# Graph convolution on one core: the last two gathered blocks of layer 1 as plain 1 KB rows, split on ScalarE and VectorE

## The chip, the cores and the metric

The kernel runs on one core of a Trainium2 chip. The metric is the device time of one execution in microseconds. TensorE is PE in the profile, VectorE DVE, ScalarE ACT, GpSimd POOL and SyncE SP.

## What is computed

Three graph-convolution layers over 6250 nodes and 100,000 edges (sorted by destination), then a residual and a layer norm:

```python
src = concat(edge_src, arange(n)); dst = concat(edge_dst, arange(n))     # with self-loops
dinv = rsqrt(segment_sum(ones, dst))                                     # 1 / sqrt(degree)
h = x                                                                    # [6250, 256] float32
for W, b in ((W1, b1), (W2, b2), (W3, b3)):                              # 256 -> 512 -> 512 -> 256
    m = (h @ W)[src] * (dinv[src] * dinv[dst])[:, None]
    h = relu(segment_sum(m, dst, n) + b)
out = layernorm(x + h)
```

Everything is float32. TensorE multiplies in a fast float32 format of fewer bits (`F32R`), so a row is split into two parts, a high one (the row rounded to `F32R`) and a low one (row minus high part); both are multiplied and added up in the accumulator.

## The kernel before

The 6250 nodes are 50 blocks of 125. A layer first aggregates rows, scaled by `dinv`, and then multiplies by its weights. A block's aggregate comes in one of two ways. **Gathered:** 16 steps each fetch 128 rows of the layer's table in HBM by an indirect DMA on GpSimd (line 1186), and a product (line 1213) adds them up by a one-hot matrix of their destinations, which VectorE builds for four products at a time (`shot`, line 1136). A 17th set of rows, shared by ten blocks, takes what is left over. **Dense:** 50 products with a matrix of edge counts between two blocks (line 1273); the counts lie as bytes and ScalarE converts them in pieces of five (line 1145). Layer 1 does blocks 0 to 21 in the dense way and 22 to 49 by gathers, with both kinds interleaved.

How layer 1 gets high and low parts of its gathered rows: blocks 22 to 25 take plain 1 KB rows and multiply them as float32. From block 26 on (`BOTH_FROM`) the rows come from a second table, `both_halves`, which holds high and low part side by side, 2 KB per row, written at the beginning of the kernel. They land in a ring of 12 tiles, `halves` (two of which hold leftover rows), and go to TensorE as they are; a tile is free when its product is done. Layers 2 and 3 gather plain rows instead and split each behind its landing, with a copy on ScalarE (line 1240) and a subtraction on VectorE (line 1243).

The order on every engine is the order of the program text; nothing reorders it, and each engine takes its instructions in turn, waiting on semaphores. The loop in `layer` sets it: one pass per gather ("step"). In step c the gather of c is put on GpSimd's queue, then the splits of rows a few steps back (`SPLIT` has for each layer how many steps later the high part, the low part and the product come), then the product of row c - `lag`, then whatever generators are due (`go`, `go_fixed`), then the dense products that fall to this step. In layer 1 `lag` is 5.

Generators carry a block on after its last product. `after1` (layer 1) scales the sum (ScalarE line 1303, VectorE 1305), transposes it (PE 1294), copies the result (ScalarE 1314), multiplies by W1 (PE 1320), adds the bias (VectorE 1325), applies relu (ScalarE 1328) and stores the rows to layer 2's table, `tab1`, through SyncE (line 74). Layer 2's first gather on GpSimd waits for the whole of `tab1`.

The generator `teams` begins layer 2's dense part while layer 1 still runs: for groups of four blocks it streams `tab1` two blocks at a time through a ring of three loads, and the counts, through SyncE (line 76; `parts<-tab`, `parts<-kept`). For each of 150 units it splits the streamed block (ScalarE line 934, VectorE 936) and converts counts (ScalarE 926), and does four pairs of matmuls (PE line 979), one pair for each of four banks of PSUM. Its loads are put in the order when layer 1 has 16 dense products left; its first pair follows when all dense blocks are ended and the four banks are free. In layer 1 two of three pairs end a step, in layer 2 nearly each.

Of the kernel before, what the change touches and what calls it, by code (L numbers as in the profile page):

```python
# [27 lines left out]
KF = 16  # L28
CAP = KF * P
GRP = 10  # L30
# [13 lines left out]
SHORT = 6  # L44
# [7 lines left out]
FEW = 22  # L52
BOTH_FROM = 26
BOTH_LAG = 5
SPLIT = ((0, 0, BOTH_LAG), (1, 2, 8), (3, 4, 9))
EXTRAS_AFTER = (3, 6, 9, 11, 13, 15, 17)
TEAM = 4
TEAMS = 3
# [338 lines left out]
def sorted_path(ctx: ExitStack, tc: tile.TileContext, x, edges, starts, found, wts, biases, room, late, out):  # L397
# [19 lines left out]
    N, C = x.shape  # L417
    HID = w1_sb.shape[2]
    EC = d.shape[1]
    NB = N // Q  # L420
# [13 lines left out]
    src = const.tile([P, NB, KF], I32, name="ssrc")  # L434
# [285 lines left out]
    MW = -(-NB * Q // 4 // 8) * 8  # L720
# [10 lines left out]
    zt2, ht2 = [room[:, room.shape[1] - n * pair:][:, :pair].rearrange("p (k v) -> p k v", v=2 * Q) for n in (2, 1)]  # L731
    wide_rows = [room[:, at:at + HID] for at in range(MW, room.shape[1] - 2 * pair - HID + 1, HID)]
    scales = wide_rows.pop()[:, :TEAM * Q]
    del wide_rows[-TEAM:]
    at = MW + len(wide_rows) * HID
    team_zt = room[:, at:at + KH * TEAM * Q].rearrange("p (k v) -> p k v", v=TEAM * Q)
# [2 lines left out]
    turn = 0  # L739
# [305 lines left out]
    def fetch(b, chunk):  # L1045
        by_rows(nc.sync, used[len(there) % 2].rearrange("p k v -> p (k v)"), kept[b])
        there.append(chunk)
# [5 lines left out]
    def layer(i, width, gathered, dense, after, rows, first=0, spacing=1.0, extras=(), filler=None, carried=None):  # L1053
# [15 lines left out]
        items = []  # L1069
# [4 lines left out]
        total = len(items)  # L1074
# [8 lines left out]
        def go_fixed(chunk):  # L1083
            for item in list(fixed):
                if item[0] <= chunk:
                    wait = next(item[1], None)
                    if wait is None:
                        fixed.remove(item)
                    else:
                        item[0] = chunk + wait  # L1090

        def go(chunk):
            for item in list(going):
                if item[0] <= chunk + late:
                    wait = next(item[1], None)
                    if wait is None:
                        going.remove(item)
                    else:
                        item[0] = chunk + late + min(wait, item[2])
# [8 lines left out]
        def sum_bank(name, most):  # L1108
            nonlocal late
            if i == 0:  # L1110
                while not common:
                    if early_copy[0]():
                        break
                    late += 1
                    go(chunk)
                return common.popleft()
            need(now, name, most)
            return idle[name].pop(0)
# [11 lines left out]
        def more_hots():  # L1130
            c0 = len(hots) * HOTS
            n = min(HOTS, len(gathered) * (KF + 1) - c0)
            if n > 0:
                at = gathered[0] * (KF + 1) + c0
                hot = onehot.tile([P, HOTS, Q], F32R, name="shot")
                nc.vector.tensor_tensor(hot[:, :n], near_cols[:, :Q].unsqueeze(1).to_broadcast([P, n, Q]),  # L1136
                                        dlo.rearrange("p b j -> p (b j)")[:, at:at + n].unsqueeze(2).to_broadcast([P, n, Q]),
                                        op=ALU.is_equal)
                hots.append(hot)
# [9 lines left out]
        landed, split_rows = {}, {}  # L1149
        hi_lag, lo_lag, lag = SPLIT[i]  # L1150

        def of_both(c):

            n, b, _ = items[c]
            return i == 0 and (n * GRP if b is None else b) >= BOTH_FROM

        def halved(c):

            return 0 <= c < total and items[c][1] is not None and i > 0
        acc = None  # L1160

        of_ten = {}
        shared, rows = rows[:2 if i == 0 else 1], rows[2 if i == 0 else 1:]
# [3 lines left out]
        def gather(c):  # L1167
            nonlocal turn
            n, b, j = items[c]
            table = both_halves if of_both(c) else tables[i]  # L1170
            if (i, b, j) == (0, BOTH_FROM, BOTH_LAG + 1):
                hot_stores.appendleft(late_hot_room)
            if b is None:
                row, at = split.popleft() if of_both(c) else shared[n % len(shared)], rest[:, n, 0:1]
                of_ten[n] = row
                if i > 0:
                    of_ten[n] = shared_halves
                    raw_of_ten.append((c, row))
            elif of_both(c):
                row, at = split.popleft(), src[:, b, j:j + 1]  # L1180
                split_rows[c] = row
            else:
                row, at = rows[turn % len(rows)], src[:, b, j:j + 1]
                (landed if i > 0 else split_rows)[c] = row
                turn += 1
            nc.gpsimd.indirect_dma_start(out=row, out_offset=None, in_=table,  # L1186
                                         in_offset=bass.IndirectOffsetOnAxis(ap=at, axis=0))
# [39 lines left out]
        with tc.manual_schedule():  # L1227
            more_hots()
            to_sum = 0
            for chunk in range(total + (SHORT if i == 1 else lag)):  # L1230
                now = chunk
                if i == 1:
                    lag = SPLIT[i][2] if returning is None else max(SHORT, SPLIT[i][2] - (chunk - returning) // 2)
                if chunk < total:
                    gather(chunk)
                if halved(chunk - hi_lag):
                    halves = split_rows[chunk - hi_lag] = split.popleft()
                    if i == 1 and halves in loaned:
                        on_loan.append(halves)
                    nc.scalar.copy(halves[:, :width], landed[chunk - hi_lag])  # L1240
                if halved(chunk - lo_lag):
                    halves = split_rows[chunk - lo_lag]
                    nc.vector.tensor_sub(halves[:, width:], landed.pop(chunk - lo_lag), halves[:, :width].bitcast(F32))  # L1243
                while to_sum <= chunk - lag:
                    product(to_sum)
                    to_sum += 1
                if raw_of_ten and to_sum >= raw_of_ten[0][0] and chunk >= raw_of_ten[0][0] + LATE:
                    row = raw_of_ten.popleft()[1]
                    nc.scalar.copy(shared_halves[:, :width], row)
                    nc.vector.tensor_sub(shared_halves[:, width:], row, shared_halves[:, :width].bitcast(F32))  # L1250
                go(chunk)
                go_fixed(chunk)
                until = min(len(dense) * NB, begun + int((chunk + 1 - first) * NB / spacing))
                if i == 0:
                    until = min(until, done + 3)
                if chunk >= total - 1:
                    until = len(dense) * NB
                while done < until:
                    m, k = divmod(done, NB)
                    if k == 0:  # L1260
                        if chunk < total - 1 and (len(there) <= m or there[m] > chunk):
                            break
                        assert len(there) > m
                        acc_d = sum_bank(bank, 3)
                        if i == 2 and m + 1 < len(dense) and len(there) == m + 1:
                            fetch(dense[m + 1], chunk)
                    if k % PIECE == 0:
                        while len(got) < min(len(dense) * CUTS, done // PIECE + 1 + ahead):
                            n, c = divmod(len(got), CUTS)
                            if n > m and (len(there) <= n or there[n] > chunk):  # L1270
                                break
                            got.append(converted(n, c))
                    nc.tensor.matmul(acc_d[:Q], lhsT=got[done // PIECE][:, k % PIECE, :], rhs=parts[:, k],  # L1273
                                     start=(k == 0), stop=(k == NB - 1))
                    products = done = done + 1
                    if k == NB - 1:
                        finished += 1
                        ended(chunk, dense[m], acc_d, bank)
            assert all(steps_ is carried for _, steps_ in fixed)
            while going:  # L1280
                late += 1
                go(chunk)
                if carried is not None:
                    next(carried)
                if filler is not None:
                    next(filler, None)
            while filler is not None and begun % PIECE:
                next(filler)
# [389 lines left out]
```

## Time and profile before

| | |
|---|---|
| time, median of 3 runs | 2076.28 us (2072.91 to 2077.11) |
| the profiled execution, its span | 2076.16 us, 2074.4 us |
| PE, PEld, DVE busy | 1923.9 us (93%), 1513.7 us (73%), 1494.1 us (72%) |
| ACT, POOL busy | 1302.3 us (63%), 1418.2 us (68%) |
| layer 1's gathers on POOL | 72.95 to 685.66 us |
| layer 2's gathers on POOL | 708.98 to 1587.99 us |
| layer 3's gathers on POOL | 1620.7 to 2060.9 us |
| gathers from `both_halves` on POOL | 384, mean 939 ns |
| all bytes moved by DMA | 486.17 MB, mean 234 GB/s |

A row of the timeline has the start, the length, engine, line, operation, output and input with shapes, and in brackets the engine's idle time before it and what ended it; rows of one kind that follow each other are merged (x2). A matmul's length runs to the end of its passage, so lengths overlap; the work that one costs is the distance to the start of the next. In a row of busy windows the first number is the length of the stretch, then come the busy times of PE, PEld, DVE, ACT and POOL with the number of instructions, PE's granted clock, the DMA engines' share and GB/s. "SPq" is the time in which SyncE issues DMAs.

### The profile page before, as it was taken

The page shows a single profiled execution, that of the slowest core. Times are in us where ns is not written, and L with a number is a line of the kernel's source. Part 1 is how long each engine was busy: PE and PEld are TensorE (multiplying, and loading weights), DVE is VectorE, ACT ScalarE, POOL GpSimd, SP SyncE. Part 2 cuts the span into 40 slices and gives each one's busy share as a digit, 9 for nine tenths or more (in the row PEclk, how much of TensorE's full clock was granted, in tenths as well). Part 3 has the DMA queues.
Part 4 walks back from the last instruction along what each step waited for, and adds up shares of the span by engine and source line. Part 5 has one row for each costly group of instructions (what it writes and reads, how often), then busy time and mean ns, then how long its engine had stood idle before and what let it go on. Part 6 is the DMA issues. An engine that isn't in the chain of part 4 may idle for free. (4 is left out here: it accounts for less than half of the span.)

```text
span 2074.4 us, 30032 instructions
## 1 busy us (share of the span) xinstructions
PE 1923.9 (93%) x8642; PEld 1513.7 (73%) x8642; DVE 1494.1 (72%) x2809; ACT 1302.3 (63%) x2484; POOL 1418.2 (68%) x1442
## 2 busy tenths in 40 slices
PE   4399999999999688999999999999989899999996
PEld 3277777777776467778888878887767777777774
DVE  6877888888882376777766777677675467777776
ACT  2576777787884465766766656667565455556553
POOL 2467777766777377777776776677674577777775
PEclk6699999999999899999999999999999999999998
DMA  7898999999999999999999998978886466666674
GB/s 172 244 308 212 271 260 256 276 260 257 275 274 252 264 268 248 269 260 265 261 262 258 258 260 239 266 230 266 244 239 189 115 180 183 182 178 190 174 191 117
DMA packets 233624, 486.17 MB, mean 234 GB/s; under 512 B 44142, under 2 KB 87358, under 8 KB 233446
## 3 DMA queue, kind: packets, MB, share of 16 engines
q0 software_dynamic: 125184, 315.61, 54.6%
q1 hardware_dynamic: 94980, 159.23, 27.9%
q10 hardware_dynamic: 13282, 9.30, 1.7%
q8 instruction: 70, 1.15, 0.2%
q14 instruction: 108, 0.88, 0.1%
HBM read 416.51 MB, written 67.47 MB: 233 GB/s over the span
## 5 line engine op out<-in xcount | busy, mean ns | idle before, releaser
L1186 POOL DMA_INDIRECT room<-tab,ssrc x1008 | 1025.8, 1018 | 384.6 <-issue 162.6
L1243 DVE TENSOR_TENSOR halves<-room,halves 128x512 fp32r<-128x512 f32 (+1 forms) x806 | 453.4, 579 | 279.0 <-ACT halves L1240 273.0
L1240 ACT CAST halves<-room 128x512 fp32r<-128x512 f32 (+1 forms) x806 | 408.5, 528 | 286.0 <-DMA room<-tab,ssrc 244.7
L1213 PE MATMUL sacc<-halves,shot 128*125 128x512 f32 x1541 | 527.1, 406 | 38.8 <-DVE shot L1136 27.8
L1186 POOL DMA_INDIRECT halves<-both,ssrc x384 | 360.5, 939 | 143.3 <-issue 41.8
L1213 PEld LDWEIGHTS sacc<-halves,shot 128*125 128x125 f32 x1541 | 286.9, 188 | 120.4 <-ACT halves L1240 25.1
L785 DVE TENSOR_TENSOR room<-near_cols,slots 128x625 bf16<-128x625 f32 (+2 forms) x435 | 325.3, 804 | 30.8 <-PE sacc L852 12.7
L1145 ACT CAST piece<-room 125x625 fp32r<-125x625 uint8 x416 | 297.2, 722 | 70.4 <-PE win_ps L1273 19.2
L1136 DVE TENSOR_TENSOR shot<-near_cols,sdlo 128x500 fp32r<-128x500 f32 x371 | 248.0, 670 | 9.3 <-PE sacc L1213 4.8
L1366 PE MATMUL win_ps<-room,w_sb 128*128 128x250 f32 (+1 forms) x832 | 192.5, 375 | 1.6 <-ACT room L1372 1.6
L1273 PE MATMUL win_ps<-parts,piece 125*125 125x512 f32 x650 | 186.2, 405 | 6.2 <-ACT piece L1145 6.2
L1273 PE MATMUL smm<-parts,piece 125*125 125x512 f32 x655 | 188.9, 405 | 1.3 <-ACT piece L1145 0.7
L1366 PEld LDWEIGHTS win_ps<-room,w_sb 128*128 128x128 f32 x832 | 158.0, 195 | 25.3 <-ACT room L1372 2.0
L1273 PE MATMUL mat_ps<-parts,piece 125*125 125x512 f32 x600 | 172.4, 404 | 1.3 <-ACT piece L1145 1.3
L852 PEld LDWEIGHTS <-room 128*125 128x125 bf16 x725 | 95.8, 138 | 74.0 <-issue 23.0
L1273 PE MATMUL sacc<-parts,piece 125*125 125x512 f32 x450 | 147.6, 432 | 0.9 <-ACT piece L1145 0.9
L1273 PEld LDWEIGHTS win_ps<-parts,piece 125*125 125x125 f32 x650 | 119.3, 188 | 37.7 <-ACT piece L1145 8.0
L814 ACT CAST room<-sacc 125x500 uint8<-125x500 f32 (+1 forms) x155 | 107.6, 712 | 56.5 <-PE sacc L852 41.7
L1273 PEld LDWEIGHTS smm<-parts,piece 125*125 125x125 f32 x655 | 116.8, 187 | 29.3 <-issue 2.3
L936 DVE TENSOR_TENSOR parts<-parts 125x512 fp32r<-125x512 f32 x150 | 103.4, 689 | 41.6 <-ACT parts L934 41.6
L1273 PEld LDWEIGHTS mat_ps<-parts,piece 125*125 125x125 f32 x600 | 107.6, 186 | 29.4 <-ACT piece L1145 3.0
L1243 DVE TENSOR_TENSOR parts<-room,parts 128x512 fp32r<-128x512 f32 x138 | 93.4, 692 | 33.3 <-ACT parts L1240 32.9
(310 smaller groups left out, 2938.5 us busy)
## 6 DMA issues: line engine op xcount, KB each, us to landing
parts<-tab SPq DMA_DIRECT2D x81, 448.0 KB
kept<-room SPq DMA_DIRECT2D x29, 683.6 KB
room<-kept SPq DMA_DIRECT2D x29, 683.6 KB
tab<-st SPq DMA_DIRECT2D x74, 224.0 KB
room<-tab,ssrc POOLq DMA_INDIRECT x1008
both<-parts SPq DMA_DIRECT2D x10, 1120.0 KB
own_row<-tab SPq DMA_DIRECT2D x38, 224.0 KB
parts<-kept SPq DMA_DIRECT2D x60, 136.7 KB
```

The source lines that it names most:

```text
L785: nc.vector.tensor_tensor(out, near_cols[:, :shape[2]].unsqueeze(1).to_broadcast(shape), numbers.unsqueeze(2).to_broadcast(shape), op=ALU. ...
L814: nc.scalar.copy(place[:, :, u * G:(u + len(ms)) * G].rearrange("p k (t r) -> p t k r", r=G), counted_in[:Q, :len(ms) * 256].rearrange("p ...
L852: nc.tensor.matmul(bank[:Q, len(pair) * 256:][:, :G * NB], lhsT=hot_lo, rhs=hot_key, start=True, stop=True)
L936: nc.vector.tensor_sub(to[:, HID:], row, to[:, :HID].bitcast(F32))
L1136: nc.vector.tensor_tensor(hot[:, :n], near_cols[:, :Q].unsqueeze(1).to_broadcast([P, n, Q]), dlo.rearrange("p b j -> p (b j)")[:, at:at + ...
L1145: convert(piece, made_or_read[:, c * PIECE:(c + 1) * PIECE, :])
L1186: nc.gpsimd.indirect_dma_start(out=row, out_offset=None, in_=table, in_offset=bass.IndirectOffsetOnAxis(ap=at, axis=0))
L1213: nc.tensor.matmul(acc[:Q, :size], lhsT=hot, rhs=row[:, c0:c0 + size], start=(i == 1 and k == c0 == 0), stop=(k == KF and c0 + size == row ...
L1240: nc.scalar.copy(halves[:, :width], landed[chunk - hi_lag])
L1243: nc.vector.tensor_sub(halves[:, width:], landed.pop(chunk - lo_lag), halves[:, :width].bitcast(F32))
L1273: nc.tensor.matmul(acc_d[:Q], lhsT=got[done // PIECE][:, k % PIECE, :], rhs=parts[:, k], start=(k == 0), stop=(k == NB - 1))
L1366: nc.tensor.matmul(h_ps[:, f, :], lhsT=w2_sb[:, k, (f2 + f) * P:(f2 + f + 1) * P], rhs=zt[:, k, :], start=(k == 0), stop=(k == KH - 1))
```

## The change

Blocks 48 and 49 (`PLAIN_FROM`) no longer come from `both_halves`: their 32 gathers fetch plain 1 KB rows of layer 1's own table into a ring of eleven rows of their own (`plain_rows`, in space that held other things earlier in the layer), ScalarE copies the high part one step later and VectorE subtracts the low part two steps later, as in layer 2, into tiles of the same `halves` ring. Products fall back from five to eight steps behind their gather over the twelve steps ahead of block 48 and come up to six again at the end; the loop runs six steps past its last gather instead of five.

```diff
 BOTH_FROM = 26
 BOTH_LAG = 5
-SPLIT = ((0, 0, BOTH_LAG), (1, 2, 8), (3, 4, 9))
+PLAIN_FROM = 48
+SPLIT = ((1, 2, BOTH_LAG), (1, 2, 8), (3, 4, 9))
...
+    plain_rows = [room[:, at:at + C] for at in range(3 * MW, MW + len(wide_rows) * HID - C + 1, C)]
...
         def of_both(c):
             n, b, _ = items[c]
-            return i == 0 and (n * GRP if b is None else b) >= BOTH_FROM
+            return i == 0 and BOTH_FROM <= (n * GRP if b is None else b) < PLAIN_FROM
 
         def halved(c):
-            return 0 <= c < total and items[c][1] is not None and i > 0
+            return 0 <= c < total and items[c][1] is not None and (i > 0 or items[c][1] >= PLAIN_FROM)
...
             else:
-                row, at = rows[turn % len(rows)], src[:, b, j:j + 1]
-                (landed if i > 0 else split_rows)[c] = row
+                ring = plain_rows if i == 0 and b >= PLAIN_FROM else rows
+                row, at = ring[turn % len(ring)], src[:, b, j:j + 1]
+                (landed if halved(c) else split_rows)[c] = row
                 turn += 1
...
-            for chunk in range(total + (SHORT if i == 1 else lag)):
+            plain = total - (NB - PLAIN_FROM) * KF
+            for chunk in range(total + (SHORT if i < 2 else lag)):
                 now = chunk
+                if i == 0:
+                    lag = min(BOTH_LAG + max(0, chunk - plain + 12) // 4, SPLIT[1][2], SHORT + max(0, total + 1 - chunk) // 2)
```

How this moves instructions is seen at two places. Lines of the changed kernel are up to six higher: its 1246 and 1249 are the splits, 1309, 1320 and 1334 the transforms on ScalarE, 1216 the products, 1300 and 1326 transposes and W1 on PE, 928 and 936 the teams' conversions, 981 their matmuls.

ScalarE, from the last dense pieces of layer 1 to the teams' first conversions (`szs`, `room`, `st`: the blocks' transforms; `parts`: the teams'), before:

```order
L1145 CAST piece<-room 125x625 x3
L1328 ACTIVATE st<-st,sdinv 125x512 x2
L1303 ACTIVATE szs<-str,sdinv 125x256
L1314 COPY room<-sacc_877 128x250
L1303 ACTIVATE szs<-smm,sdinv 125x256
L934 CAST parts<-parts 125x512
L926 CAST parts<-parts 125x5x125 x4
L1328 ACTIVATE st<-st,sdinv 125x512
L1314 COPY room<-sacc_877 128x250
```

The same place now:

```order
L1334 ACTIVATE st<-st,sdinv 125x512
L1246 CAST halves_858<-room 128x256
L1246 CAST halves_860<-room 128x256
L1309 ACTIVATE szs<-str,sdinv 125x256
L1246 CAST halves_861<-room 128x256
L936 CAST parts<-parts 125x512
L928 CAST parts<-parts 125x5x125 x2
L1246 CAST halves_862<-room 128x256
L928 CAST parts<-parts 125x5x125 x2
L1246 CAST halves_863<-room 128x256
L1320 COPY room<-sacc_876 128x250
L936 CAST parts<-parts 125x512
```

Copies of gathered rows now stand between the transforms and between the teams' conversions; one relu has gone from behind the first conversions.

TensorE, where the teams' first pair stands (`win_ps` is block 49's sum before; now `sacc_877` is block 48's and `sacc_876` block 49's), before:

```order
L1294 MATMUL sacc_877<-ident_r,szs 128x125 x2
L1213 MATMUL win_ps<-halves_863,shot 125x512
L1213 MATMUL win_ps<-halves_864,shot 125x512
L1320 MATMUL sacc_876<-w_58,room 125x512
L979 MATMUL sacc_878<-parts 128x500 x2
L1213 MATMUL win_ps<-halves_865,shot 125x512
L1320 MATMUL sacc_876<-w_58,room 125x512
L979 MATMUL mat_ps<-parts 128x500 x2
```

And now:

```order
L1300 MATMUL sacc_876<-ident_r,szs 128x125 x2
L1216 MATMUL sacc_877<-halves_855,shot 125x512
L1216 MATMUL sacc_877<-halves_856,shot 125x512
L1326 MATMUL win_ps<-w_58,room 125x512
L981 MATMUL sacc_878<-parts 128x500 x2
L1216 MATMUL sacc_877<-halves_857,shot 125x512
L1326 MATMUL win_ps<-w_58,room 125x512
L981 MATMUL mat_ps<-parts 128x500 x2
L1216 MATMUL sacc_877<-halves_858,shot 125x512
L1216 MATMUL sacc_877<-halves_866,shot 125x512
L981 MATMUL smm<-parts 128x500 x2
L1201 MATMUL sacc_876<-parts,ident_r 125x512
```

The first pair has moved from among block 49's products to among block 48's: two products of block 48 and all sixteen of block 49 now stand behind it, where eleven of block 49 did.

## The prediction, made before the change was run

> **What bounds the kernel now.** I read the page first, then the busy windows around the change of layers, then each engine's timeline there. The profiled execution took 2076.16 us: its span of 2074.4 and 1.8 around it. The median of the three timed runs is 2076.28, so a sum made against the profiled time needs no correction. About 0.2% (4.15 us) is what a measurement of this kernel can tell from no change.
>
> ```profile
> span 2074.4 us, 30032 instructions
> ```
>
> Stretches of 5 us at the end of layer 1 and the start of layer 2 (columns: PE, PEld, DVE, ACT, POOL busy with counts; granted PE clock; DMA share; GB/s):
>
> ```profile
> 665.00:670.00 5.00, 4.62 (x22) 3.42 (x21) 1.35 (x3) 0.77 (x2) 3.78 (x5) 1.00 1.08 272
> 670.00:675.00 5.00, 3.43 (x12) 1.67 (x10) 1.48 (x3) 0.55 (x2) 3.78 (x5) 1.00 1.36 264
> 675.00:680.00 5.00, 0.79 (x1) 0.28 (x1) 0.69 (x1) 1.94 (x4) 3.78 (x5) 0.69 1.35 255
> 680.00:685.00 5.00, 2.94 (x5) 1.73 (x6) 1.28 (x2) 3.04 (x6) 1.28 (x2) 0.50 1.38 273
> ```
>
> TensorE is the bound up to 668 us. Then it starves, with the DMA engines over-booked (shares of 1.35 and more). The PE timeline says on what, and shows a second hole at 710:
>
> ```profile
> 652.27 0.40 PE L1213 MATMUL smm<-halves,shot 128*125 128x512 f32 x1
> ...
> 667.47 0.64 PE L1273 MATMUL str<-parts,piece 125*125 125x512 f32 x2
> ...
> 673.94 0.49 PE L1213 MATMUL win_ps<-halves,shot 128*125 128x512 f32 x1 [1.00 <-DMA halves<-both,ssrc]
> 677.01 0.79 PE L1213 MATMUL win_ps<-halves,shot 128*125 128x512 f32 x1 [2.57 <-DMA halves<-both,ssrc]
> 682.05 2.07 PE L1320 MATMUL sacc<-w,room 128*125 128x512 f32 x2 [4.26 <-ACT room L1314]
> 683.14 1.82 PE L979 MATMUL sacc<-parts 125*128 125x500 f32 x2
> ...
> 695.91 0.63 PE L1213 MATMUL win_ps<-halves,shot 128*125 128x512 f32 x2
> ...
> 708.85 0.61 PE L979 MATMUL smm<-parts 125*128 125x500 f32 x2
> 709.30 0.62 PE L979 MATMUL str<-parts 125*128 125x500 f32 x2
> 718.98 1.51 PE L979 MATMUL sacc<-parts 125*128 125x500 f32 x2 [9.05 <-ACT parts L934]
> ```
>
> 652.27 is the first product of the 32 gathers that change, 667.47 the last of layer 1's dense products, 683.14 the first matmul of the teams (they begin layer 2's dense part early), 695.91 layer 1's last product. POOL's rows give those gathers, from 641.68 to 685.66:
>
> ```profile
> 641.68 0.94 POOL L1186 DMA_INDIRECT halves<-both,ssrc  x1 [0.30 <-issue]
> 642.92 0.94 POOL L1186 DMA_INDIRECT halves<-both,ssrc  x1 [0.31 <-PE win_ps L1273]
> ...
> 666.97 0.94 POOL L1186 DMA_INDIRECT halves<-both,ssrc  x1 [0.30 <-PE smm L1213]
> 668.22 0.94 POOL L1186 DMA_INDIRECT halves<-both,ssrc  x1 [0.31 <-PE str L1273]
> ...
> 685.66 0.94 POOL L1186 DMA_INDIRECT halves<-both,ssrc  x1 [3.47 <-DMA parts<-tab]
> 708.98 0.96 POOL L1186 DMA_INDIRECT room<-tab,rest  x1 [22.39 <-DMA tab<-st]
> ```
>
> The two products that waited for DMA belong, by count, to the gathers of 666.97 and 668.22: 7.0 and 8.8 us from issue to use. Layer 2's first gather, 708.98, waits for the last store of layer 1's table. What lies between 678 and 709 is on ScalarE and SyncE:
>
> ```profile
> 678.06 0.62 ACT L934 CAST parts<-parts 125x512 fp32r<-125x512 f32 x1 [7.45 <-DMA parts<-tab]
> 678.58 2.55 ACT L926 CAST parts<-parts 125x625 fp32r<-125x625 uint8 x4
> 681.04 0.71 ACT L1328 ACTIVATE st<-st,sdinv 125x512 f32<-125x512 f32 x1
> 681.66 0.34 ACT L1314 COPY room<-sacc 128x250 f32<-128x250 f32 x1
> ```
>
> ```profile
> 664.48 4.19 SPq L76 DMA_DIRECT2D parts<-kept  x8
> 668.72 4.31 SPq L76 DMA_DIRECT2D parts<-tab  x6
> ```
>
> So the chain is: SyncE issues the teams' loads from 664.48; the first load of layer 1's table (issued 668.72) lands only at 678.06; ScalarE stands before it for 7.45 us, then converts four pieces (2.46), and only behind these comes the copy (681.66) for which TensorE waits until 682.05. From 683.14 TensorE works through to the last product at 695.91. From that product to layer 2's first gather it is 13.1 us.
>
> **The change part by part.** *Bytes.* At a gather every 1.24 us (641.68, 642.92), 128 rows of 2 KB are 211 GB/s; with 1 KB rows half of that, 4.2 MB less in all. From 664.48 to 678.06 the teams' loads (8 transfers of counts, 0.61 MB, then 0.50 MB of the table) moved 1.11 MB, 82 GB/s. With 264 GB/s in all (row of 670) and 105 for gathers, 159 are left, and the 1.11 MB take 7.0 us: landing at 671.5. That leaves out the table's own stores, which SyncE issues just ahead of the loads; two of them (0.26 MB each, 125 rows of 2 KB) make it 1.63 MB and 674. Nothing reaches much below 670.8, for the load is issued only at 668.72 (0.7 us sooner at best) and the shortest passage that I find, below, is 2.8 us. At the other end, 678.06 stays if halved rows relieve nothing. I take 672.5, between the two that come from the rows of this very stretch.
>
> Whether rows of half the length take half of the engines' time, two other layers tell (2 KB rows at 1000 us, 1 KB rows at 1700 us), and the row of 1500 is for later:
>
> ```profile
> 1000.00:1050.00 50.00, 50.00 (x229) 41.97 (x228) 37.14 (x61) 33.30 (x60) 36.77 (x36) 1.00 0.92 254
> 1500.00:1550.00 50.00, 40.48 (x164) 31.52 (x163) 38.63 (x62) 32.25 (x61) 36.80 (x36) 0.90 0.88 250
> 1700.00:1750.00 50.00, 50.00 (x217) 39.89 (x215) 36.37 (x97) 27.73 (x66) 38.42 (x39) 1.00 0.70 184
> ```
>
> A full share would be 276 GB/s in the one and 263 in the other, so nearly by the byte. The Trainium skill ("DMA: Bandwidth & Descriptors", section "Anatomy of one DMA — SWDGE (gpsimd) path") speaks against the change here: a transfer issued by GpSimd costs a fixed 2.0 us and only its bytes at 436 GB/s on top. By that rule, as an estimate, a gather of 0.26 MB goes from 2.6 to 2.3 us; if that is the engines' time, their load falls by 12% and not by half, the teams' load lands about when it did, and the time is that of the second rival (2081.9) instead of 2074.4. The two rows speak against reading the fixed part as time that the engines are taken.
>
> *Splits.* There are 32 copies on ScalarE and 32 subtractions on VectorE more. Layer 3 has the same instructions:
>
> ```profile
> L1243 DVE TENSOR_TENSOR halves<-room,halves 128x256 fp32r<-128x256 f32 x336 | 136.1, 420 | 110.2 <-ACT halves L1240 108.4 <-PE mat_ps L1273 0.7 <-PE smm L1273 0.5
> L1240 ACT CAST halves<-room 128x256 fp32r<-128x256 f32 x336 | 126.9, 401 | 100.3 <-DMA room<-tab,ssrc 89.2 <-DVE halves L1243 5.3 <-DVE szs L1412 1.7
> ```
>
> That is 12.8 us on ScalarE and 13.4 on VectorE over some 45 us in which they are idle for more than half (0.55 to 3.04 and 0.69 to 1.48 of 5 us): the busy time costs nothing. What could cost is their order. ScalarE takes row c one step behind its gather, so everything behind it on ScalarE (pieces L1145 for the dense products, the transforms L1303, L1314, L1328) and on VectorE (the one-hots L1136, L1325) now waits for that row. How late a 1 KB row can be, layer 3 shows: a gather in its middle and its last one, and the copies for which ScalarE waited for them (paired by counting):
>
> ```profile
> 1801.17 1.01 POOL L1186 DMA_INDIRECT room<-tab,ssrc  x1 [0.30 <-DVE szs L1411]
> ...
> 2060.90 0.95 POOL L1186 DMA_INDIRECT room<-tab,ssrc  x1 [0.30 <-issue]
> ```
>
> ```profile
> 1808.46 0.41 ACT L1240 CAST halves<-room 128x256 fp32r<-128x256 f32 x1 [2.79 <-DMA room<-tab,ssrc]
> ...
> 2063.72 0.41 ACT L1240 CAST halves<-room 128x256 fp32r<-128x256 f32 x1 [0.82 <-DMA room<-tab,ssrc]
> ```
>
> So 7.3 us in traffic and 2.8 at the end without. A one-hot made at step c stands behind the subtraction of row c-2, so TensorE's step c comes no sooner than issue(c) - 2.5 + 2.8 to 7.3 + 0.40 + 0.42 + 0.67, that is 1.8 to 6.3 us behind the gather. TensorE is behind it by more already: at 652.27 it is in the sixth of these steps, whose gather was issued at 641.68 + 5 x 1.24 = 647.9 (4.4 us), at 667.47 in the sixteenth, issued at 660.3 (7.2 us). Only at the beginning, and only with late rows, does 6.3 exceed 4.4: some 2 us at most, which then stay, as TensorE has no slack up to 668. Against it, products eight steps behind instead of five put three of them (0.23 each) behind the dense end, 0.7 us sooner there. I set the two against each other: 0 (bounds -0.7 and +2).
>
> *POOL.* It no longer waits for a free row of the split ring: the plain rows have a ring of eleven of their own, free once subtracted. Its last gather moves from 685.66 to about 641.68 + 31 x 1.24 = 680.2, and a landing of 7.3 still brings the row before 688. That is before TensorE gets to it, so it gains nothing.
>
> *Order.* The teams start earlier in the order, and more of their work stands ahead of the last product: counted in PE's order, 23 pairs of L979 between the first and the last product against 16, 21 products against 12, and two L1320 more. A pair is 0.45 us (708.85, 709.30), a product 0.23, an L1320 0.46: 3.2 + 2.1 + 0.9 = 6.2 us more. ScalarE's way from the landed load to the first pair was 683.14 - 678.06 = 5.1; it loses one L1328 (0.62) and gains two copies (0.80): 5.3. So the last product comes at 672.5 + 5.3 + (695.91 - 683.14) + 6.2 = 696.8, against 695.91. Layer 2 starts 0.9 us later, within -0.8 and +2.4 by the bounds of the landing (670.8 and 674).
>
> What is won is work. By PE's order 63 pairs against 54 stand ahead of layer 2's first product, and TensorE now waits for that product anyway (9.05 us at 709.30). So 9 pairs, 9 x 0.45 = 4.1 us, leave layer 2, where each step carries about one pair until the teams end. All of it counts where TensorE never idles (the row of 1000: 50.00 of 50), nothing where it idles more than that (the row of 1500, just behind the teams' end: 40.48 of 50). Between 0 and 4.1 I take 2.7, nearer to the row without idle time, since most of the teams' steps lie in such stretches.
>
> *Sum.* 2076.16 + 0.9 (start of layer 2) - 2.7 (pairs) = **2074.4**. Bounds: -0.8 - 4.1 gives 2071.3, +2.4 with nothing from the pairs 2078.6.
>
> **The rivals.** *Everything lands well (2068.9).* The first load lands at 670.8 (start of layer 2 -0.8), all nine pairs count (-4.1), and the clock stays up: 683.14 to 695.91 is 12.8 us for 10.4 us of work (16 pairs, 12 products, one L1320), so 2.4 us went to the lowered clock (0.50 in the row of 680). If the products that now come at the gathers' pace of 1.24 us keep TensorE awake, they come back. 2076.16 - 0.8 - 4.1 - 2.4 = 2068.9. For it: twenty products run unhindered where before they stood for DMA. Against it: one product of 0.23 us in 1.24 is little activity.
>
> *The load lands no sooner (2081.9, slower).* If the teams' first load still lands at 678.06, because the engines are as full as before, then the larger amount of work ahead of the last product is pure delay: 678.06 + 5.3 + 12.8 + 6.2 = 702.3 against 695.91, 6.4 us later. Engines so full mean late rows too, so the 2 us of the splits come with it; the pairs give back 2.7: 2076.16 + 6.4 + 2.0 - 2.7 = 2081.9. It decides from a landing of 674.3 on, where delay and pairs cancel. For it: shares of 1.35 to 1.38 from 670 to 685 say that far more was queued than could be served, and layer 3's landing of 7.3 us came at a mere 0.70. Against it: 105 GB/s less are asked for.
>
> **How the numbers follow.** The forecast has 0.50: by its bounds of 2071.3 to 2078.6 mostly within 0.2%, with 0.08 below 2072.0. The first rival has 0.24, all of it faster. The second has 0.26, slower (beyond 2080.3). That makes faster 0.32, same 0.42, slower 0.26. The range goes from 2067.5 (the first rival, with 1.4 for a sooner start of the loads) to 2082.0, the second rival's price; what lies beyond that price, about half of its chance, and a small part of the first are left out.
>
> **What would show it.** Right: POOL issues the 32 gathers at 1.24 to 1.31 us without a gap, the last by 682.5; ScalarE's first L936 of the teams (L934 before) starts at 671 to 674 instead of 678.06; the first pair comes near 678 and the last product near 697, with no wait for gathered rows on PE between; layer 2's first gather is within 2 us of 708.98; the teams' last pair comes some 2 to 4 us sooner than before. Wrong: a ScalarE wait for a gathered row of over 5 us ahead of a piece or a transform, dense products that end later than 669, or a first load that lands behind 674.3. I would be wrong altogether if layer 2 then took another course, since its order against the teams shifts by nine pairs.

## The result, and the profile after

The changed kernel takes 2091.22 us (median; 2088.54 to 2101.12) where the kernel before takes 2076.19 in the same measurement: a ratio of 1.0083, 95% interval 1.0067 to 1.0099. It is slower, and outside the forecast's range. The profiled execution took 2093.96 us.

```profile
span 2092.3 us, 30116 instructions
```

First the end of layer 1, at which the prediction looked. The four stretches of 5 us again, of the changed kernel:

```profile
665.00:670.00 5.00, 4.61 (x21) 3.23 (x19) 3.74 (x8) 2.46 (x6) 3.78 (x5) 1.00 0.89 244
670.00:675.00 5.00, 0.15 (x1) 0.00 (x0) 0.00 (x0) 1.80 (x4) 3.78 (x5) 0.94 1.05 254
675.00:680.00 5.00, 2.80 (x5) 1.59 (x6) 3.45 (x7) 4.29 (x12) 3.78 (x5) 0.50 1.05 253
680.00:685.00 5.00, 5.00 (x19) 3.55 (x18) 3.17 (x7) 2.68 (x7) 2.35 (x3) 0.88 1.04 289
```

The DMA share fell from 1.35 and more to 1.05. ScalarE's timeline (the teams' first conversion), TensorE's (last dense products, first pair, last product) and GpSimd's (first and last of the 32 gathers, layer 2's first):

```profile
673.20 0.62 ACT L936 CAST parts<-parts 125x512 fp32r<-125x512 f32 x1 [3.91 <-DMA parts<-tab]
```

```profile
667.53 0.64 PE L1279 MATMUL str<-parts,piece 125*125 125x512 f32 x2
...
678.28 1.82 PE L981 MATMUL sacc<-parts 125*128 125x500 f32 x2
...
697.81 0.63 PE L1216 MATMUL sacc<-halves,shot 128*125 128x512 f32 x2
```

```profile
642.73 0.95 POOL L1189 DMA_INDIRECT room<-tab,ssrc  x1 [0.31 <-issue]
...
682.01 0.94 POOL L1189 DMA_INDIRECT room<-tab,ssrc  x1 [0.30 <-issue]
709.03 1.04 POOL L1189 DMA_INDIRECT room<-tab,rest  x1 [26.07 <-DMA parts<-tab]
```

All of this is as predicted, and layer 2 starts at 709.03 instead of 708.98. The time is lost later, in code that the change does not touch. GpSimd's timeline at the end of layer 2's gathers, the start of layer 3's and their end:

```profile
1614.60 1.27 POOL L1189 DMA_INDIRECT room<-tab,ssrc  x1 [0.53 <-DVE halves L1249]
1641.51 0.94 POOL L1189 DMA_INDIRECT room<-tab,rest  x1 [25.64 <-issue]
...
2079.74 0.95 POOL L1189 DMA_INDIRECT room<-tab,ssrc  x1 [0.30 <-issue]
```

Layer 2's 612 gathers go from 709.03 to 1614.60, 905.6 us, against 879.0 before: 26.6 us more. The gap to layer 3 gives 5.8 back (26.9 against 32.7) and layer 3 itself 2.0 (438.2 against 440.2); with layer 2's start that is 18.8 at the last gather (2079.74 against 2060.90) and 17.9 of span.

### The profile page after: what moved, and what is told of

The parts are those of the page before. It is cut to its first block, busy times and chain, and to the rows that moved or that the text cites. A ratio compares the mean times of both kernels' runs of the same rounds, so it can differ in the third digit from the quotient of the medians.

```text
span 2092.3 us, 30116 instructions
## 1 busy us (share of the span) xinstructions
PE 1930.7 (92%) x8642; PEld 1517.6 (73%) x8642; DVE 1508.0 (72%) x2841; ACT 1313.7 (63%) x2516; POOL 1428.0 (68%) x1442
## 4 chain that ended last, share of the span: by engine, by line
PE 56%; DMA 17%; issue 9%; DVE 5%; POOL 5%; ACT 4%; SPq 1%; ACTq 0%; POOLq 0%; DVEq 0%
DMA room<-tab,ssrc 15%; PE sacc L1216 10%; PE win_ps L1279 6%; PE smm L1279 6%; PE mat_ps L1279 5%; POOL room L1189 5%; PE sacc L1279 5%; PE win_ps L1372 4%; PE win_ps L1385 3%; PE sacc L1326 2%; DVE halves L1249 1%; PE sacc L854 1%; PE str L1279 1%; ACT halves L1246 1%; PE str L981 1%
## 5 line engine op out<-in xcount | busy, mean ns | idle before, releaser
L1189 POOL DMA_INDIRECT room<-tab,ssrc x1040 | 1066.5, 1025 | 409.5 <-issue 168.8
L1249 DVE TENSOR_TENSOR halves<-room,halves 128x512 fp32r<-128x512 f32 (+1 forms) x841 | 467.7, 573 | 302.4 <-ACT halves L1246 296.8
L1246 ACT CAST halves<-room 128x512 fp32r<-128x512 f32 (+1 forms) x841 | 422.5, 524 | 288.3 <-DMA room<-tab,ssrc 257.6
L1216 PE MATMUL sacc<-halves,shot 128*125 128x512 f32 x1581 | 544.0, 409 | 49.5 <-DVE shot L1138 36.8
L1189 POOL DMA_INDIRECT halves<-both,ssrc x352 | 330.5, 939 | 128.1 <-issue 40.3
L1216 PEld LDWEIGHTS sacc<-halves,shot 128*125 128x125 f32 x1581 | 296.2, 190 | 133.4 <-ACT halves L1246 21.8
```

The lines of the kernel that those rows point to most:

```text
L1216: nc.tensor.matmul(acc[:Q, :size], lhsT=hot, rhs=row[:, c0:c0 + size], start=(i == 1 and k == c0 == 0), stop=(k == KF and c0 + size == row ...
```

## Experiments

Ratios are against the kernel before, each with its 95% interval. The traces come from several chips, so times are compared through the ratios. A = changed kernel, B = kernel before.

**Which part of the change does it?** Two things pass from layer 1 into layer 2: the teams stand nine pairs further on, and the ring of gathered rows begins at another row.

*hold5*: A with the teams' first pair put back.

```diff
         half(1, 1)
+        yield 5
         pairs_done = 0
```

> The changed kernel with the teams' first pair held back by five steps, so that 54 pairs stand ahead of layer 2's first product and 16 ahead of layer 1's last, as in the kernel before (the changed kernel: 63 and 23). Theory A (the loss in layer 2 comes from the teams standing nine pairs further on against layer 2's blocks): the loss goes, 2072 to 2078 us, layer 2's gathers take about 879 us from first to last. Theory B (it comes from the ring of gathered rows, which enters layer 2 at position 5 of 7 instead of 1): it stays, 2088 to 2095 us, gathers about 905 us. Theory C (contention at the end of layer 1 or of the transfers): 2088 to 2095 us too, but the next run tells it from B.

Measured: 0.9981 (0.9967 to 0.9995), 2071.87 us, a hair below theory A's range; layer 2's gathers take 875.2 us.

*a_turn* and *b_turn*: the ring's count, at the end of layer 1, put back in A and advanced in B.

```diff
 assert len(common) == 7 - TEAM
+turn -= 2 * KF      # a_turn;  in b_turn: turn += 2 * KF
```

> The changed kernel with the count of the ring of gathered rows set back by 32 before layer 2, so that layer 2 begins at the same one of its 7 rows as in the kernel before; the teams stay nine pairs ahead. Theory A (the teams' place): nothing changes, 2088 to 2095 us. Theory B (the ring's place): the loss goes, 2072 to 2080 us. Theory C: 2088 to 2095 us.

> The kernel before with the count of the ring advanced by 32 before layer 2, so that layer 2 begins at the row at which the changed kernel begins; the teams stand as before. Theory A: 2074 to 2079 us. Theory B: 2088 to 2095 us. Theory C: 2074 to 2079 us.

Measured: a_turn 1.0086 (1.0064 to 1.0108), b_turn 0.9986 (0.9969 to 1.0002). The ring has no part in it.

*b_p2*: B with the teams alone moved ahead.

```diff
-if in_layer == 0 and pairs_done % 3 or ...
+if in_layer == 0 and pairs_done % 2 or ...
```

> The kernel before with a step between the teams' pairs of layer 1 that is taken after every odd pair instead of after two of three: 66 pairs instead of 54 stand ahead of layer 2's first product and 21 instead of 16 ahead of layer 1's last. Theory A: slower, 2083 to 2095 us, with layer 2's gathers 890 us or longer. Theory B: 2072 to 2078 us, since 12 pairs leave layer 2 and 5 x 0.45 us come into layer 1's end. Theory C: 2074 to 2079 us.

Measured: 1.0103 (1.0066 to 1.0140), 2091.76 us; layer 2's gathers take 898.9 us. So a loss of this size comes without plain rows, without splits and without another lag, as soon as the teams are further on. Theory A holds, B and C fall. It does not say how.

**Is it the distance, or a phase?** Over hundreds of steps a constant distance of nine pairs should cost nothing, so I tried a phase between the teams' conversions and the blocks (theory P) against plain distance (theory M).

*a_d2* and *h5_d1*: a pause of the teams in layer 2, two steps in A, one step in hold5.

```diff
         for u, (g, k) in enumerate(units):
+            if in_layer == 1 and now >= EAGER and not paused:
+                paused = True
+                yield 2      # h5_d1: yield 1
```

> The changed kernel with the teams paused once, for two steps, at step 9 of layer 2; layer 1 stays as the change has it. The teams are then 6.6 steps ahead of where they stand in the kernel before, instead of 8.6. Theory M (the further the teams are ahead of layer 2's blocks, the more layer 2 loses): about a quarter of the loss goes, 2086 to 2090 us. Theory P (what counts is where in a block's 16 steps the teams' five-unit conversions on ScalarE fall; they come every 19.17 steps, so five of them fill six blocks at places 3.2 steps apart, and two steps bring the places back to those of before): the loss goes, 2070 to 2080 us.

> The changed kernel with the first pair held back by five steps (2071.9 us) and the teams paused once more, for one step, at step 9 of layer 2. Theory M: as fast as without the pause or faster, 2068 to 2074 us. Theory P: the conversions fall one step off, as in the changed kernel, 2084 to 2092 us.

*a_k1*: A with the conversions of counts one unit earlier. *hold9*: hold5 with nine steps.

```diff
-if k % PIECE == 2 and u + PIECE < len(units):
+if k % PIECE == 1 and u + PIECE < len(units):      # a_k1
```

> The changed kernel with the teams' five-unit conversions, and the loads of counts behind them, one unit (four pairs, 3.8 steps) earlier, and nothing else moved; the pairs stand as far ahead as the change has them. Theory M: 2088 to 2095 us. Theory P: the places in the block move by 3.8 modulo 3.2 = 0.6 step, a part of the loss goes, 2075 to 2088 us.

> The changed kernel with the first pair held back by nine steps instead of five: 48 pairs ahead of layer 2's first product. Theory M: as fast as with five or faster, 2066 to 2073 us. Theory P: the conversions fall 0.65 step off the good places, 2072 to 2085 us.

Measured: a_d2 1.0018 (1.0000 to 1.0036), h5_d1 0.9976 (0.9958 to 0.9993), a_k1 1.0102 (1.0080 to 1.0125), hold9 0.9956 (0.9940 to 0.9972; 2064.81 us). Theory P is out: only a_d2 (2078.81 us) lies in its range, while h5_d1 (2068.48) should have been slow and a_k1 (2092.53) better. Theory M does not fit either: two steps of nearly nine took away most of the loss (from 1.0083 to 1.0018). Something between them decides.

**Where the time goes.** I listed the distances between the starts of layer 2's gathers, 1.44 us in the mean before. Those over 4.5 us, by the number of the gather behind which they lie:

| kernel | ratio | distances over 4.5 us (gather: us) |
|---|---|---|
| B, hold5, h5_d1, hold9, b_turn, a_d2 | 0.9956 to 1.0018 | none |
| A | 1.0083 | 240: 6.5, 369: 7.8, 560: 5.0 |
| a_turn | 1.0086 | 240: 6.8, 369: 7.8, 560: 5.0 |
| a_k1 | 1.0102 | 17: 11.8, 240: 7.8, 369: 10.8 |
| b_p2 | 1.0103 | 21: 6.8, 182: 4.6, 439: 6.0, 560: 5.8 |

A's three places on GpSimd's timeline:

```profile
1058.46 0.94 POOL L1189 DMA_INDIRECT room<-tab,ssrc  x1 [0.94 <-DVE halves L1249]
1064.99 0.95 POOL L1189 DMA_INDIRECT room<-tab,ssrc  x1 [5.58 <-DVE halves L1249]
...
1254.28 0.94 POOL L1189 DMA_INDIRECT room<-tab,ssrc  x1 [0.87 <-DVE halves L1249]
1262.07 0.95 POOL L1189 DMA_INDIRECT room<-tab,ssrc  x1 [6.85 <-DVE parts L1249]
...
1537.74 0.95 POOL L1189 DMA_INDIRECT room<-tab,ssrc  x1 [0.30 <-issue]
1542.76 0.94 POOL L1189 DMA_INDIRECT room<-tab,ssrc  x1 [4.07 <-DVE halves L1249]
```

They exceed three ordinary distances by 15.0 us, of the 26.6 that layer 2 lost. GpSimd waits for VectorE to free a row. The timeline of all engines at the second place, in order of time, says why VectorE is late. Lines 1372 and 1378 are the products with W2 and the relu of `hidden`, the generator that carries two aggregated blocks through W2 and W3; 1352 copies a transposed block of layer 2:

```profile
1252.67 0.62 ACT L1246 CAST halves<-room 128x512 fp32r<-128x512 f32 x1 [0.82 <-DMA room<-tab,ssrc]
1253.19 0.82 ACT L1378 ACTIVATE room<-win_ps,b_sb 128x250 f32<-128x250 f32 x2
1253.32 0.69 DVE L1249 TENSOR_TENSOR halves<-room,halves 128x512 fp32r<-128x512 f32 x1 [1.29 <-ACT halves L1246]
1254.07 1.96 PE L1372 MATMUL win_ps<-room,w_sb 128*128 128x250 f32 x8 [1.62 <-ACT room L1378]
1254.28 0.94 POOL L1189 DMA_INDIRECT room<-tab,ssrc  x1 [0.87 <-DVE halves L1249]
1255.86 0.59 PE L1300 MATMUL sacc<-ident_r,szs 125*128 125x125 f32 x4
1256.29 1.86 PE L1372 MATMUL win_ps<-room,w_sb 128*128 128x250 f32 x8
1258.18 0.83 ACT L1378 ACTIVATE room<-win_ps,b_sb 128x250 f32<-128x250 f32 x2 [4.17 <-PE win_ps L1372]
1258.90 1.05 ACT L1352 COPY room<-sacc 128x500 f32<-128x500 f32 x2
1259.54 0.73 PE L1216 MATMUL sacc<-halves,shot 128*125 128x512 f32 x2 [1.39 <-ACT room L1352]
1259.83 0.64 ACT L936 CAST parts<-parts 125x512 fp32r<-125x512 f32 x1
...
1260.35 1.69 ACT L1246 CAST parts<-room 128x512 fp32r<-128x512 f32 x3
1260.51 0.69 DVE L938 TENSOR_TENSOR parts<-parts 125x512 fp32r<-125x512 f32 x1 [6.50 <-ACT parts L936]
...
1261.12 0.69 DVE L1249 TENSOR_TENSOR parts<-room,parts 128x512 fp32r<-128x512 f32 x1
...
1262.07 0.95 POOL L1189 DMA_INDIRECT room<-tab,ssrc  x1 [6.85 <-DVE parts L1249]
```

ScalarE stands for 4.17 us before a relu whose matmuls TensorE is only then doing. Behind it on ScalarE, in turn, are the copies of gathered rows (1260.35, three of them at once: they had landed). VectorE stands for 6.50 us: its next instruction needs the teams' copy (1259.83), which is in ScalarE's queue behind the relu and two copies more. Only then does it subtract a gathered row (1261.12) and so free it, and GpSimd has stood for 6.85. That ScalarE's queue is strictly first in, first out is what the Trainium skill says ("PSUM — Partial Sum Buffer", section "Engine vs sequencer instructions"), and these rows agree: nothing passed the relu in 4.17 us.

Why the relu stands so close behind its matmuls is seen in the order of the instructions. TensorE at the first of the three places, changed kernel (the timeline above, of the second, counts each W2 product twice):

```
L981 MATMUL sacc_878<-parts 128x500 x2
L1216 MATMUL sacc_877<-halves_6268,shot 125x512 x2
L1216 MATMUL sacc_877<-halves_6264,shot 125x512 x2
L1372 MATMUL win_ps<-room,w_sb 128x250 x4
L981 MATMUL mat_ps<-parts 128x500 x2
L1372 MATMUL win_ps<-room,w_sb 128x250 x4
L1300 MATMUL sacc_877<-ident_r,szs 128x125 x4
L1372 MATMUL win_ps<-room,w_sb 128x250 x8
L1216 MATMUL sacc_876<-halves_6269,shot 125x512 x2
```

An ordinary place, kernel before: between two groups of W2 products stand a gathered product and a pair.

```
L1366 MATMUL win_ps<-room,w_sb 128x250 x4
L979 MATMUL sacc_878<-parts 128x500 x2
L1213 MATMUL sacc_877<-parts,shot 125x512 x2
L1366 MATMUL win_ps<-room,w_sb 128x250 x4
L979 MATMUL mat_ps<-parts 128x500 x2
L1213 MATMUL sacc_877<-parts,shot 125x512 x2
```

In A the transforms run through several rounds with no row, product or pair between. The code does that here, when a block's first product finds no free sum bank (layer 2 has two):

```python
while held.get(name, 0) >= most:
    late += 1
    go(chunk)          # (comment added) only the transforms; no gather, no split, no pair
```

And the banks are missing because of `hidden`. The teams' results go through it, two blocks at a time, six times in all, and so do layer 2's own blocks, two every 32 steps. It has one tile for what comes out of W2, `ht2`, which a pair of blocks takes first and keeps to its end, and one window bank. Counted in the order, the teams' results come in B at steps 152, 216, 344, 408, 536 and 568, seven to nine steps behind layer 2's own (143, 208, 337, 401, 528, 560). In A they come at 143, 207, 335, 392, 527 and 554: at 207, 335 and 527 a step or two *ahead* of layer 2's own, which then wait for `ht2` (the pair of step 208 has it at 229, in B at 213) and keep `zt2`, their place ahead of it. The next block's sum waits for that place in its bank, the block after it takes the second bank, and a third finds none. The layer stands for 9, 8 and 9 steps at its steps 234, 363 and 554. GpSimd's long distances end at gathers 241, 370 and 561, seven later: there are seven rows in the ring. In hold5, h5_d1, hold9 and a_d2 the layer nowhere stands, in a_turn and a_k1 as in A, in b_p2 for 16 steps at five places (5, 1, 4, 1 and 5). I call this theory W; where the texts below speak of the one window bank, it is `ht2` and that bank together.

**Theory W tried both ways.** *a_tz11*, *a_tz17*: A, in which only the teams' six results begin later; the pairs stay nine ahead. *b_tz25*: B, in which only these come later, so that they fall just ahead of layer 2's own.

```diff
             if n == TEAM - 1:
...
-                yield SOON
+                for _ in range(11):      # a_tz17: 17;  b_tz25, in B: 25
+                    yield 1
                 team_ended[0](hidden(groups[g][:2], ...))
```

The loop takes the place of a wait of two steps, so the first result of each group comes 9, 15 and 23 steps later.

> The changed kernel with the teams' six results (hidden of two blocks at a time) begun eleven steps later, at steps 152, 216, 344, 408, 536 and 568 of layer 2 as in the kernel before, instead of 143, 207, 335, 392, 527 and 554; the pairs stay nine ahead. Theory W (at 207, 335 and 527 a team's result takes the one window bank one or two steps ahead of layer 2's own two blocks, those keep both sum banks, and the layer stands at its next block for 9, 8 and 9 steps of the order in which no row is gathered): the loss goes, 2066 to 2076 us, and the jumps at steps 240 and 370 with it. Theory M (the pairs' place itself): 2088 to 2095 us.

> The changed kernel with the teams' six results begun seventeen steps later (steps 158, 222, 350, 414, 542, 574, as they stand in the kernel held back by nine steps, 2064.8 us). Theory W: the loss goes, 2062 to 2075 us. Theory M: 2088 to 2095 us.

> The kernel before with the teams' six results begun 23 steps later and nothing else changed: they then stand at steps 175, 231, 367, 424, 559 and 587, a step or two ahead of layer 2's own pairs of blocks at 176, 369 and 560, and the layer stands for 9, 8 and 5 steps at steps 202, 395 and 586. Theory W: slower by 12 to 24 us, 2086 to 2098 us, with jumps of 4 us or more in the gathers near steps 207 and 400. Theory M: 2072 to 2079 us, since no pair moves.

Measured: a_tz11 0.9988 (0.9970 to 1.0007; 2074.06 us), a_tz17 1.0003 (0.9984 to 1.0022; 2076.73 us, a little above its range), b_tz25 1.0090 (1.0055 to 1.0124; 2093.04 us). GpSimd's waits from 709 to 1600 us (in total, number, the longest), of A:

```profile
POOL room L1189 <- DVE halves L1249: 80.8, 108, 5.6
POOL room L1189 <- DVE parts L1249: 26.7, 36, 6.9
```

and of a_tz11:

```profile
POOL room L1190 <- DVE halves L1250: 66.7, 111, 2.6
POOL room L1190 <- DVE parts L1250: 24.0, 41, 2.0
```

The long waits are gone, no distance is over 3.9 us, and layer 2's gathers take 881.2 us (GpSimd's timeline, a_tz11):

```profile
706.79 1.03 POOL L1190 DMA_INDIRECT room<-tab,rest  x1 [26.26 <-DMA parts<-tab]
...
1588.02 0.95 POOL L1190 DMA_INDIRECT room<-tab,ssrc  x1 [0.31 <-issue]
```

b_tz25 has them, at the two places that were named ahead (gathers 208 and 401) and, seven gathers behind its third stand at 586, at 592. On GpSimd's timeline:

```profile
1003.66 0.95 POOL L1187 DMA_INDIRECT room<-tab,ssrc  x1 [0.30 <-issue]
1010.35 1.15 POOL L1187 DMA_INDIRECT room<-tab,ssrc  x1 [5.75 <-DVE halves L1244]
...
1287.39 0.95 POOL L1187 DMA_INDIRECT room<-tab,ssrc  x1 [0.30 <-issue]
1294.04 1.15 POOL L1187 DMA_INDIRECT room<-tab,ssrc  x1 [5.70 <-DVE halves L1244]
...
1565.78 0.95 POOL L1187 DMA_INDIRECT room<-tab,ssrc  x1 [0.30 <-issue]
1572.22 1.15 POOL L1187 DMA_INDIRECT room<-tab,ssrc  x1 [5.49 <-DVE halves L1244]
```

A fourth, 5.8 us behind gather 463, lies at no stand; B has a lesser one there, 4.4 us.

So the kernel before can be made as slow as the changed one by the place of six results, and the changed one as fast as before. Theory M falls: no pair moved in any of the three.

*hold14*: A with the first pair fourteen steps later, to see whether more holding back gains more.

> The changed kernel with the first pair held back by fourteen steps: 42 pairs ahead of layer 2's first product and 2 ahead of layer 1's last, so that the teams' results fall clear of layer 2's own (163, 227, 355, 419, 547, 579). Theory W: no loss, and layer 1's end keeps what nine pairs fewer give it, 2060 to 2072 us. Theory M: 2060 to 2068 us, further down than with nine steps (2064.8 us).

Measured: 0.9986 (0.9965 to 1.0007), 2072.96 us, 1.0 above W's range and 5.0 above M's, and no better than hold9. By pairs ahead the kernels without a stand read 42: 0.9986, 48: 0.9956, 54: 0.9981, 63: 0.9988 (a_tz11): no trend shows. The lowest ratio of all is that of hold9, the change with the first pair nine steps later: it is faster than A and B, but its interval meets those of hold5 and hold14.

## Why the prediction was wrong, point by point

- *Bytes.* Right. The first load landed for 673.20, forecast 672.5 between 670.8 and 674. (The upper bound should have been 674.7: 1.63 MB at 159 GB/s take 10.2 us from 664.48.) Of the 4.9 us won, 1.6 come from an earlier issue, at 667.15 instead of 668.72, where the prediction saw 0.7 at best. The rest is passage: from SyncE's issue to ScalarE's first conversion, which waits for the load, it is 6.1 us instead of 9.3. That goes with the plain rows: it is 8.5 to 9.6 us in the four kernels with 2 KB rows (B, b_turn, b_p2, b_tz25) and 5.9 to 7.3 in the ten with 1 KB rows. The moment alone does not tell: hold9, with 1 KB rows, converts only at 676.84, since its load is issued at 670.55. Three of the fourteen, with SyncE's row and ScalarE's, in this order: b_turn, b_p2 and a_turn.

```profile
667.33 4.82 SPq L76 DMA_DIRECT2D parts<-tab  x6
676.95 0.62 ACT L934 CAST parts<-parts 125x512 fp32r<-125x512 f32 x1 [7.86 <-DMA parts<-tab]
```

```profile
667.22 4.00 SPq L76 DMA_DIRECT2D parts<-tab  x6
675.95 0.62 ACT L934 CAST parts<-parts 125x512 fp32r<-125x512 f32 x1 [6.95 <-DMA parts<-tab]
```

```profile
663.34 3.10 SPq L77 DMA_DIRECT2D parts<-tab  x6
669.68 0.62 ACT L936 CAST parts<-parts 125x512 fp32r<-125x512 f32 x1 [4.88 <-DMA parts<-tab]
```

The rule from the Trainium skill ("DMA: Bandwidth & Descriptors", section "Anatomy of one DMA — SWDGE (gpsimd) path"), read as time that the engines are taken, would have left that passage near 9.3 us; it took 6.1, so the trace does not agree with that reading.
- *Splits.* Right: the last dense products are at 667.53 against 667.47, and ScalarE nowhere idles for more than 3.13 us before the copy of one of these rows. One reading was off: in the row of 680 ScalarE was busy for 3.04 of 5 us, so it was not idle for more than half there. That cost nothing.
- *POOL.* Right: 642.73 to 682.01, 1.27 us each, no gap.
- *Order, first half.* Right within 1 us: first pair 678.28 (678), last product 697.81 (696.8), layer 2's start 0.05 later (0.9). TensorE waits for no gathered row between the first pair and the last product.
- *Order, second half: "What is won is work."* **This step failed.** It took the nine pairs as work that leaves layer 2, worth between 0 and 4.1 us, and so put a floor of nothing under them; a loss was left out of the bounds for no reason that the profile gave. What the pairs also do is bring the teams' results forward by nine steps, past layer 2's own, to `ht2` and the one window bank. In place of -2.7 stood +17.8 (the 17.9 of span, less the 0.05 by which layer 2 began later), and a_tz11 takes away all of it that can be measured. The sign given for this step did not come either: the teams' last pair starts at 1491.22 instead of 1479.97, 11 us later and not 2 to 4 sooner.
- *The rest of the sum* agrees when that is taken out, but is not shown: 2074.4 over 2076.16 is 0.9992, a_tz11 measured 0.9988, and its interval holds no change at all as well. The -2.7 finds no support: hold5, with no more pairs ahead than B, is no slower than a_tz11. In a_tz11 the teams' last pair does come 7.5 us sooner than in B, counted from layer 2's first gather (1470.24 from 706.79; 1479.97 from 708.98), and still layer 2's gathers take 881.2 us against 879.0.
- *Rivals.* Neither came about. The second gave a slower kernel, but its mechanism (a load that lands no sooner) did not occur. The last sentence of the prediction names the shift of layer 2's order against the teams as a way to be altogether wrong, without working it out; it had neither a price nor a chance.
- *What stays open.* The three long distances are 15.0 of the 26.6 us of layer 2. Gather by gather, A is 1.3 us behind a_tz11 at gather 235, ahead of the first of them, and 24.3 at the last gather; 15.4 of that come at the three distances and 7.6 little by little behind them, and why these last was not traced. Nor do stands explain the other slow kernels in full. b_p2's three longer ones would make the distances behind gathers 176, 369 and 560 long, and only the last is (1.8, 2.0 and 5.8 us); a_k1's largest, behind 17, lies at no stand, and its stand at 554 costs nothing (2.2 us behind 560). b_p2 is thus tied to the teams' place, but not to its stands. a_d2 nowhere stands and is still between hold5 and A (1.0018), and why hold9 is the best of those that don't stand is not known.

## What to carry to other kernels

Where the order is written out ahead and shared banks are handed out by turn, an edit that moves work by a few steps must be followed to the end of the program, not of the stage that it is in: look in the order for places where a stage's transforms stand together with nothing between them. A queue that takes its instructions in turn makes such a place expensive, since one relu 4 us early in ScalarE's queue held up splits, rows and gathers that had nothing to do with it. When a stage without a changed line gets slower, list the distances between its regular instructions first: three outliers say more than totals of waits.

## What the runs showed of the hardware

The stand does not show on TensorE's clock, but on the DMA engines, just behind it (busy windows of A, at the second place):

```profile
1255.00:1260.00 5.00, 3.61 (x19) 2.88 (x18) 0.00 (x0) 1.81 (x5) 0.22 (x1) 1.00 0.72 237
1260.00:1265.00 5.00, 5.00 (x24) 4.07 (x23) 4.49 (x8) 4.63 (x9) 2.32 (x3) 1.00 0.20 55
```

The clock stays at 1.00 while TensorE is busy for 3.61 of 5 us; the rate of all transfers falls to 55 GB/s, from some 250. No gather was issued for 7.8 us, and at the ordinary 1.44 us gathers of 0.26 MB are, by estimate, 182 GB/s of the rate. At the other two places the rate falls to 123 (1060 to 1065) and 59 GB/s (1540 to 1545). That a wait of 4 us on ScalarE would leave the DMA engines a share of 0.20 I had not expected.
